# Four graph layers on one core: sums over features in quarters of the array, serial segment maxima, a softmax in two parts

## The chip, the core and the metric

The kernel runs on one core of a Trainium2 chip. The metric is the device time of one execution in microseconds (us); the number quoted is the median of three runs. TensorE appears as PE (matmuls) and PEld (weight loads), VectorE as DVE, ScalarE as ACT, GpSimd as POOL, SyncE as SP. Everything is float32 (f32), but for the operands of one matmul, which are float32r.

## The reference

The input `x` has 128 graphs of 64 nodes with 256 features each. Four layers follow one another, each as `x = layernorm(x + layer(x))`:

```python
# layer 0: dense attention over the 64 nodes of a graph
e = leaky(s1[:, :, None] + s2[:, None, :]); e = where(adj == 0, -inf, e)
h = softmax(e) @ Wh                       # Wh = x @ W, s1 = Wh @ a1, s2 = Wh @ a2
# layer 1: attention over 512 edges, 4 heads
e = einsum('behd,hd->beh', leaky(Xq[:, src] + Xq[:, dst]), a) + log(adj[src, dst] + eps)
m = segment_max(e, src); ex = exp(e - m[src])
attn = ex / segment_sum(ex, src)[src]
Y = segment_sum(attn * Xv[:, dst], src) @ W_out.T
# layer 2: graph convolution, then 256 -> 512 -> 256 with batch norm over all tokens
# layer 3: two graph convolutions, then LSTMs over windows of 1, 2, 3, 4 nodes
```

The change is in layers 0 and 1, and in the helper that normalises.

## The kernel before

The 128 graphs are cut in 16 blocks `q` of 8 graphs. A block is four tiles of 128 partitions, two graphs in each. A first long loop works through the blocks and does layers 0 and 1, and the first matmul of layer 2, in steps that are interleaved by hand: while block `q` passes through the edge attention (`l1_graph`, eight times, once per graph), block `q + 2` passes through layer 0 (`l0_a` to `l0_e`), block `q + 1` through its projections (`l1_t`, `l1_qv`), and block `q - 3` through the weighted sum and the output of layer 1 (`v_a`, `v_b`, `v_c`). The kernel is written against a layer that orders each engine's instructions itself and sets the semaphores; each engine then runs its own instructions strictly in that order.

For one graph `l1_graph` gathers the query sums of 512 edges by a matmul into `z` (L322; 128 features of a half on the partitions, 512 edges along the row), ACT applies a relu into `u` (L324), DVE joins the two halves with the signs of `a` (L325). `reduce_heads` (L312) then sums over the features, head by head: a matmul with a matrix `apad` that is zero but for four columns, so that the four head sums of this graph land on the right four of the 128 rows of one PSUM bank, `e`. The matmul is 128 columns wide although only four are not zero. Sixteen such matmuls, two blocks, fill the 16 x 4 = 64 used rows of `e`; the queue `pend` lets each run two graphs late (`DEEP = 2`).

Every two blocks (a softmax group `S`) `l1_softmax` adds the linear part of the scores (L335, a matmul with `spad`) and the edge bias, and finds the maximum over each segment of equal `src` along the row with two scans: one forward (`up`, L340), one backward (`dn`, L341), both over `e`, joined by a maximum (L342). After the exponential (L344) two more scans make the segment sums (L347, L348). PE transposes both results (L353), DVE divides (L357, L359), and four indirect DMAs (L363) from POOL's queue scatter the weights into a table in DRAM, from which the dense matrices `ld` are read back (L369). `v_a` rearranges them on POOL into `am` (L377) and multiplies them with the values in 64x64 corners of the array (L384).

In layer 0, `sb` (L227) is the column of scores `s2` broadcast along a row of 128, made on POOL; PE transposes it (L233), and DVE adds the other score and the mask into `lr` (L236) and takes the leaky relu into `e0` (L239).

`layernorm` takes statistics on DVE, computes the inverse root on POOL (L82), negates the mean into `ln_ng` on DVE (L94) and applies both in one instruction per row group on the given engine (L96). After the loop, the last three blocks' `v_a`, `v_b`, `v_c` are interleaved with layer 2's first matmuls (`up_block`, L684). The rest, layer 2's second half and layer 3 with its LSTMs, is some two thirds of the time and touched only through `layernorm`.

Of the kernel before, what the change touches and what calls it, by code (L numbers as in the profile page):

```python
# [8 lines left out]
F32 = mybir.dt.float32  # L9
F32R = mybir.dt.float32r  # L10
I32 = mybir.dt.int32
AF = mybir.ActivationFunctionType
# [5 lines left out]
P = 128  # L18
NB = 128
N = 64  # L20
# [9 lines left out]
GQ = 8  # L30
BPS = 2
SROWS = BPS * GQ * HEADS
PAIRS = N * N
SKIP = 4
NEG = -1.0e30
# [5 lines left out]
def kernel(ctx: ExitStack, tc: tile.TileContext, i, out):  # L41
# [42 lines left out]
    def layernorm(dst, src, n, engine):  # L84

        st = small.tile([P, n, 6], F32, name="ln_st", bufs=6)
        mv = small.tile([P, n, 2], F32, name="ln_mv", bufs=6)
        ng = small.tile([P, n], F32, name="ln_ng", bufs=6)
        rs = small.tile([P, n], F32, name="ln_rs", bufs=6)
        for r in range(n):  # L90
            nc.vector.bn_stats(st[:, r, :], src[:, r, :])
            nc.vector.bn_aggr(mv[:, r, :], st[:, r, :])
        rsqrt(rs, mv[:, :, 1], n)
        nc.vector.tensor_scalar_mul(ng, mv[:, :, 0], -1.0)  # L94
        for r in range(n):
            engine.tensor_scalar(dst[:, r, :], src[:, r, :], ng[:, r:r + 1], rs[:, r:r + 1],  # L96
                                 op0=OP.add, op1=OP.mult)


    bd = const.tile([P, P], F32, name="bd")  # L100
# [10 lines left out]
    with ExitStack() as two:  # L111
# [62 lines left out]

        mask = wa.tile([P, P], F32, name="mask")
        aht = wa.tile([P, P], F32, name="aht")
        apad = wa.tile([P, 2 * P - HEADS], F32, name="apad")
        same = wa.tile([P, 1], F32, name="same")
        gath = wa.tile([P, E], F32, name="gath")
        gath_r = wa.tile([P, E], F32R, name="gath_r")  # L180
# [35 lines left out]
        def l0_b(q):  # L216
            xT = L0[q]["xT"]
            wh = L0[q]["wh"] = own(q, [P, PQ, D + 2], "wh")
            for c in range(PQ):
                p_ = bank([D + 2])  # L220
                for k in range(KD):
                    nc.tensor.matmul(p_, xT[:, k, c * P:(c + 1) * P], w0[:, k, :],  # L222
                                     start=k == 0, stop=k == KD - 1)
                nc.scalar.activation(wh[:, c, :], p_, AF.Copy)

            sb = L0[q]["sb"] = own(q, [P, PQ, P], "sb")
            nc.gpsimd.tensor_copy(sb, wh[:, :, D + 1:].to_broadcast([P, PQ, P]))  # L227

        def l0_c(q):
            wh, sb = L0[q]["wh"], L0[q]["sb"]  # L230
            sc = bank([PQ, P])
            for c in range(PQ):
                nc.tensor.transpose(sc[:, c, :], sb[:, c, :], ident)  # L233
            t = own(q, [P, PQ, P], "lr")
            for c in range(PQ):
                nc.vector.scalar_tensor_tensor(t[:, c, :], sc[:, c, :], wh[:, c, D:D + 1], mask,  # L236
                                               op0=OP.add, op1=OP.add)
            e = L0[q]["e"] = work.tile([P, PQ, P], F32, name="e0")
            nc.vector.scalar_tensor_tensor(e, t, SLOPE, t, op0=OP.mult, op1=OP.max)  # L239
            mx = small.tile([P, PQ], F32, name="mx")  # L240
            nc.vector.tensor_reduce(mx, e, AX.X, OP.max, negate=True)
            sm = small.tile([P, PQ], F32, name="sm")
            for c in range(PQ):
                nc.scalar.activation(e[:, c, :], e[:, c, :], AF.Exp, bias=mx[:, c:c + 1],
                                     accum_out=sm[:, c:c + 1])
            ri = L0[q]["ri"] = small.tile([P, PQ], F32, name="ri")
            nc.vector.reciprocal(ri, sm)
# [31 lines left out]

        def l1_qv(q, c2):  # L280
            xT, v = L1[q]["xT"], L1[q]["v"]
            sp = spads[q // BPS % 2].rearrange("p (s b c h) -> p s b c h", s=4, b=BPS, c=PQ)
            pv = bank([2, D])
            for c in (2 * c2, 2 * c2 + 1):
                pq = bank([D + HEADS])
                for k in range(KD):
                    nc.tensor.matmul(pq, xT[:, k, c * P:(c + 1) * P], wq[:, k, :],  # L287
                                     start=k == 0, stop=k == KD - 1)
                for k in range(KD):
                    nc.tensor.matmul(pv[:, c % 2, :], xT[:, k, c * P:(c + 1) * P], wv[:, k, :],  # L290
                                     start=k == 0, stop=k == KD - 1)

                qs = work.tile([P, 2, D], F32R, name="qs", bufs=6)
                L1[q]["qs"].append(qs)
                for s in range(2):
                    r, ro = slice(s * N, (s + 1) * N), slice((1 - s) * N, (2 - s) * N)
                    nc.scalar.activation(qs[r, s, :], pq[r, :D], AF.Copy)  # L297
                    nc.vector.tensor_sub(qs[ro, s, :], pq[r, :D], qs[r, s, :].bitcast(F32))  # L298
                    nc.scalar.activation(sp[r, s, q % BPS, c, :], pq[r, D:], AF.Copy, scale=SLOPE)
            nc.scalar.activation(v[:, 2 * c2:2 * c2 + 2, :], pv, AF.Copy)  # L300

        pes, pend = {}, []
        DEEP = 2

        def reduce_heads(q, b, t):
            S = q // BPS
            c, s = divmod(b, 2)
            r0 = ((s * BPS + q % BPS) * PQ + c) * HEADS
            first = q % BPS == 0 and b == 0
            if first:  # L310
                pes[S] = bank([E], name="e", bufs=1)
            nc.tensor.matmul(pes[S], apad[:, P - HEADS - r0:2 * P - HEADS - r0], t, start=first, stop=False)  # L312

        def l1_graph(q, b):

# [4 lines left out]
            z = bank([KD, E], name="z", bufs=2)  # L320
            for k in range(KD):
                nc.tensor.matmul(z[:, k, :], L1[q]["qs"][c][:, s, k * P:(k + 1) * P], gath_r, start=True, stop=True)  # L322
            u = work.tile([P, KD, E], F32, name="u", bufs=4)
            nc.scalar.activation(u, z, AF.Relu)  # L324
            nc.vector.scalar_tensor_tensor(u[:, 0, :], u[:, 1, :], same, u[:, 0, :], op0=OP.mult, op1=OP.add)  # L325
            pend.append((q, b, u[:, 0, :]))
            if len(pend) > DEEP:
                reduce_heads(*pend.pop(0))

        ld = {}  # L330

        def l1_softmax(S):

# [3 lines left out]
            nc.vector.tensor_add(e, pe, lb)  # L337
            up = vp.tile([P, E], F32, name="up")
            dn = vp.tile([P, E], F32, name="dn")
            nc.vector.tensor_tensor_scan(up, seg[:, :E], e, NEG, OP.add, OP.max)  # L340
            nc.vector.tensor_tensor_scan(dn[:, ::-1], seg[:, 1:][:, ::-1], e[:, ::-1], NEG, OP.add, OP.max)  # L341
            nc.vector.tensor_max(up, up, dn)  # L342
            nc.vector.tensor_sub(e, e, up)
            nc.scalar.activation(e, e, AF.Exp)  # L344


            nc.vector.tensor_tensor_scan(up, keep, e, 0.0, OP.mult, OP.add)  # L347
            nc.vector.tensor_tensor_scan(dn[:, ::-1], seg[:, 1:][:, ::-1], up[:, ::-1], NEG, OP.add, OP.max)  # L348
            rows = []
# [4 lines left out]
                rows.append(p_)  # L354
            at = vp.tile([P, EC, SROWS], F32, name="at")
            rd = vp.tile([P, EC, SROWS], F32, name="rd")
            nc.vector.reciprocal(rd, rows[1][:, :, :SROWS])  # L357
            for c in range(EC):
                nc.vector.scalar_tensor_tensor(at[:, c, :], rows[0][:, c, :SROWS], count[:, c:c + 1], rd[:, c, :],  # L359
                                               op0=OP.mult, op1=OP.mult)  # L360

            for c in range(EC):
                nc.gpsimd.indirect_dma_start(  # L363
# [8 lines left out]
        def v_a(q):  # L372
            S, b = divmod(q, BPS)
            v = L1[q]["v"]
            am = vp.tile([P, PQ * HEADS, N], F32, name="am", bufs=2)
            w = PQ * HEADS
            nc.gpsimd.tensor_copy(am, ld[S][:, :, b * w:(b + 1) * w].rearrange("p n r -> p r n"))  # L377
            pY = [bank([KD, PQ, N]) for _ in range(2)]
            for c in range(PQ):
                for h in range(HEADS):  # L380
                    for s in range(2):
                        r = slice(s * N, (s + 1) * N)
                        r0 = (h % 2) * 64
                        nc.tensor.matmul(pY[s][r0:r0 + 64, h // 2, c, :], v[r, c, h * 64:(h + 1) * 64],  # L384
                                         am[r, c * HEADS + h, :], start=True, stop=True)
            yT = L1[q]["yT"] = vp.tile([P, KD, PQ, 2, N], F32, name="yT")
            for s in range(2):
                nc.scalar.activation(yT[:, :, :, s, :], pY[s], AF.Copy)
# [1 line left out]
        def v_b(q):  # L390
# [3 lines left out]
            for c2 in range(2):  # L394
# [3 lines left out]
                        nc.tensor.matmul(p_[:, c, :], yT[:, k, 2 * c2 + c].rearrange("p s n -> p (s n)"),  # L398
                                         wout[:, k, :], start=k == 0, stop=k == KD - 1)
                nc.vector.tensor_add(y[:, 2 * c2:2 * c2 + 2, :], p_, x1[:, 2 * c2:2 * c2 + 2, :])  # L400
            x2 = L1[q]["x2"] = vp.tile([P, PQ, D], F32, name="x2")
            layernorm(x2, y, PQ, nc.gpsimd)
            nc.sync.dma_start(x2_dram[q], x2.rearrange("p c d -> p (c d)"))

# [94 lines left out]
        def setup_signs():  # L499
# [1 line left out]
            nc.vector.tensor_scalar(acol, acol, 0.0, -2.0, op0=OP.is_lt, op1=OP.mult)  # L501
            nc.vector.tensor_scalar_add(acol, acol, 1.0)
            nc.vector.tensor_mul(same, acol[:, 0:1], acol[:, 1:2])
            nc.vector.tensor_scalar_mul(apad, iota_e[:, :2 * P - HEADS], 0.0)
            for h in range(HEADS):
                r, c0 = slice(h * 32, (h + 1) * 32), P - HEADS + h
                nc.vector.tensor_copy(apad[r, c0:c0 + 1], acol[r, 0:1])

        l0_a(0)
# [113 lines left out]
        for q in range(NQ):  # L623
# [10 lines left out]
            ]  # L634
            for b in range(GQ):
                some(l1_graph, q, b)
                if q and q % BPS == 0 and b == DEEP - 1:
                    l1_softmax(q // BPS - 1)
                for step, n, *more in between[b]:
                    some(step, n, *more)  # L640
                if setup:
                    setup.pop(0)()
        while pend:
            reduce_heads(*pend.pop(0))
        l1_softmax(NQ // BPS - 1)
        ph.close()


# [404 lines left out]
```

## Time and profile before

The median of three runs is 2236.68 us (2236.19 to 2237.63). The profiled execution spans 2237.3 us.

| what | value |
|---|---|
| PE busy | 2163.4 us (97%) |
| DVE busy | 926.0 us (41%) |
| ACT busy | 944.6 us (42%) |
| POOL busy | 435.0 us (19%) |
| chain that ended last: PE | 81% |
| chain that ended last: DVE, ACT | 9%, 5% |
| loop over blocks with all steps | about 60 to 595 us of the span |
| layer 2 and the LSTM part | from about 665 us on |

A group of instructions in the profile is given as line, engine, operation, output tile and input tiles, shapes and count; then busy time, mean duration in nanoseconds of one, and the idle time of the engine just before such instructions with what ended it. An f32 matmul appears as two instructions. Matmuls overlap their neighbours, so the durations of matmuls add up to more than the time they take; the distance from one start to the next is the honest price.

### The profile page before, as it was taken

What the parts mean: (1) busy time and instruction counts of PE and PEld (TensorE: products, weight loads), DVE (VectorE), ACT (ScalarE), POOL (GpSimd) and SP (SyncE); (2) the same over time, 40 slices, a digit from 0 to 9 for tenths busy, and PEclk for the clock granted to TensorE, in tenths of its full rate; (3) what the DMA queues carried; (4) which work ended last, traced back from release to release, by engine and by line L of the source; (5) the groups of instructions that cost most, each with busy time, mean ns of one, the idle gap of its engine ahead of it and who ended that gap; (6) DMA issues with size and microseconds to landing.
All of it is one profiled execution on the core that took longest, in us unless ns stands there. A gap on an engine that the chain in (4) does not pass through costs nothing.

```text
span 2237.3 us, 27559 instructions
## 1 busy us (share of the span) xinstructions
PE 2163.4 (97%) x10675; PEld 1411.7 (63%) x10675; DVE 926.0 (41%) x2136; ACT 944.6 (42%) x1821; POOL 435.0 (19%) x561
## 2 busy tenths in 40 slices
PE   5989999999899998999999999999999999999998
PEld 4667676666554444468468468468468468568467
DVE  7576756666544435232232323323323323323212
ACT  2655665656334802343343333333433433433333
POOL 1133334333320002011111111112112112112002
PEclk8999999999999998999999999999999999999999
DMA  4021233202223003000000000001001001000001
GB/s 121 19 40 29 50 50 51 50 32 39 41 41 111 19 0 104 0 20 29 29 20 29 29 19 29 29 20 29 29 19 29 28 20 29 19 10 29 10 0 29
DMA packets 129266, 74.46 MB, mean 33 GB/s; under 512 B 84976, under 2 KB 119920, under 8 KB 128880
## 3 DMA queue, kind: packets, MB, share of 16 engines
q1 hardware_dynamic: 124528, 70.74, 13.0%
q8 instruction: 84, 1.38, 0.3%
q10 hardware_dynamic: 3584, 0.92, 0.2%
q0 software_dynamic: 1024, 1.05, 0.2%
q14 instruction: 46, 0.38, 0.1%
HBM read 44.12 MB, written 28.57 MB: 32 GB/s over the span
## 4 chain that ended last, share of the span: by engine, by line
PE 81%; DVE 9%; ACT 5%; POOL 2%; DMA 1%; issue 1%; ACTq 0%; SPq 0%; POOLq 0%; DVEq 0%
PE l L927 34%; PE l L933 19%; PE pz L749 5%; PE pz L684 4%; DVE u L325 3%; PE g L867 2%; PE g L879 2%; PE e L312 2%; PE m L287 2%; PE m L222 2%; PE m L398 1%; PE g L829 1%; ACT u L324 1%; PE m L410 1%; PE m L290 1%
## 5 line engine op out<-in xcount | busy, mean ns | idle before, releaser
L927 PE MATMUL l<-H,wih 128*128 128x256 f32 (+2 forms) x2496 | 792.7, 470 | 0.8 <-ACT gate_g L947 0.5
L927 PEld LDWEIGHTS l<-H,wih 128*128 128x128 f32 x2496 | 467.7, 190 | 273.7 <-issue 179.4
L933 PE MATMUL l<-hid,whh 128*128 128x256 f32 (+2 forms) x1536 | 435.9, 437 | 0.0
L933 PEld LDWEIGHTS l<-hid,whh 128*128 128x128 f32 x1536 | 291.9, 190 | 128.4 <-issue 61.2
L939 ACT ACTIVATE gate_i<-l,bias 128x256 f32<-128x256 f32 (+2 forms) x176 | 100.0, 568 | 522.7 <-PE l L933 468.7
L942 DVE TENSOR_TENSOR gate_i<-gate_i,gate_g 128x256 f32<-128x256 f32 (+2 forms) x96 | 47.8, 498 | 580.8 <-ACT gate_g L939 580.8
L943 POOL TENSOR_TENSOR cell<-gate_f,cell 128x256 f32<-128x256 f32 (+2 forms) x96 | 83.6, 871 | 903.8 <-ACT gate_f L939 903.8
L82 POOL TENSOR_TENSOR ln_rs<-ln_rs,mhalf 128x2 f32<-128x2 f32 (+2 forms) x97 | 79.5, 819 | 498.7 <-DVE ln_ng L94 497.6
L324 ACT ACTIVATE u<-z 128x1024 f32<-128x1024 f32 x128 | 129.5, 1024 | 59.4 <-PE z L322 58.8
L312 PE MATMUL e<-u,apad 128*128 128x512 f32 x256 | 133.1, 606 | 11.3 <-DVE u L325 9.9
L939 ACT ACTIVATE gate_g<-l,bias 128x256 f32<-128x256 f32 (+2 forms) x176 | 100.1, 569 | 99.1 <-PE l L927 49.9
L325 DVE SCALAR_TENSOR_TENSOR u<-u,same 128x512 f32<-128x512 f32 x128 | 106.3, 841 | 57.8 <-ACT u L324 56.9
L939 ACT ACTIVATE gate_o<-l,bias 128x256 f32<-128x256 f32 (+2 forms) x176 | 99.2, 564 | 64.1 <-PE l L933 54.1
L946 DVE TENSOR_TENSOR cell<-gate_i,gate_g 128x512 f32<-128x512 f32 (+2 forms) x80 | 48.3, 603 | 156.1 <-ACT gate_g L939 155.6
L947 ACT ACTIVATE gate_g<-cell 128x256 f32<-128x256 f32 (+2 forms) x176 | 89.9, 511 | 52.9 <-DVE cell L946 38.4
L684 PE MATMUL pz<-A,w 128*128 128x512 f32 x256 | 112.1, 594 | 0.0
L322 PE MATMUL z<-gath_r,qs 128*128 128x512 f32 x256 | 106.9, 499 | 0.5 <-DVE qs L298 0.3
L684 PEld LDWEIGHTS pz<-A,w 128*128 128x128 f32 x256 | 48.1, 190 | 56.4 <-issue 54.3
L952 DVE TENSOR_TENSOR H<-gate_o,gate_g 128x512 f32<-128x512 f32 (+1 forms) x64 | 40.9, 639 | 89.0 <-PE l L927 71.4
L298 DVE TENSOR_TENSOR qs<-m,qs 64x256 fp32r<-64x256 f32 x128 | 54.1, 423 | 54.9 <-ACT qs L297 53.3
L939 ACT ACTIVATE gate_f<-l,bias 128x256 f32<-128x256 f32 (+2 forms) x96 | 51.0, 531 | 59.7 <-PE l L933 59.7
L287 PE MATMUL m<-wq,tT 128*128 128x260 f32 x256 | 71.2, 396 | 3.7 <-ACT tT L202 3.2
(240 smaller groups left out, 2674.8 us busy)
## 6 DMA issues: line engine op xcount, KB each, us to landing
xin<-in_x SPq DMA_DIRECT2D x16, 512.0 KB
ld<-table SPq DMA_DIRECT2D x16, 512.0 KB
x_dram<-x SPq DMA_DIRECT2D x16, 512.0 KB
x2r<-x_dram SPq DMA_DIRECT2D x32, 256.0 KB
x_dram<-A SPq DMA_DIRECT2D x64, 128.0 KB
x3r<-x_dram SPq DMA_DIRECT2D x64, 128.0 KB
out<-st SPq DMA_DIRECT2D x64, 128.0 KB
wih<-in_WihT SPq DMA_DIRECT2D x3, 1024.0 KB
```

The costliest lines, as they stand in the source:

```text
L287: nc.tensor.matmul(pq, xT[:, k, c * P:(c + 1) * P], wq[:, k, :], start=k == 0, stop=k == KD - 1)
L312: nc.tensor.matmul(pes[S], apad[:, P - HEADS - r0:2 * P - HEADS - r0], t, start=first, stop=False)
L322: nc.tensor.matmul(z[:, k, :], L1[q]["qs"][c][:, s, k * P:(k + 1) * P], gath_r, start=True, stop=True)
L324: nc.scalar.activation(u, z, AF.Relu)
L325: nc.vector.scalar_tensor_tensor(u[:, 0, :], u[:, 1, :], same, u[:, 0, :], op0=OP.mult, op1=OP.add)
L684: nc.tensor.matmul(p_, w1[:, k, m * P:(m + 1) * P], A[:, q, k * QT:(k + 1) * QT], start=k == 0, stop=k == KD - 1)
L749: nc.tensor.matmul(p_, w2[:, k, m * P:(m + 1) * P], hidden(q, k), start=k == 0, stop=k == M1 - 1)
L927: nc.tensor.matmul(gates[n], wih[p][:, k, mw * P:(mw + 1) * P], Hw[:, k, :, s, :], start=k == 0, stop=not s and k == KD - 1)
L933: nc.tensor.matmul(gates[n], whh[p][:, k, m * P:(m + 1) * P], hid[:, k], start=False, stop=k == KD - 1)
L939: nc.scalar.activation(act[n], gates[n], AF.Tanh if n == "g" else AF.Sigmoid, bias=bias[:, p - 1, m:m + 1])
L943: nc.gpsimd.tensor_tensor(cell[:, j], act["f"], cell[:, j], OP.mult)
L947: nc.scalar.activation(act["g"], cell[:, j], AF.Tanh)
```

## The change

Six edits are made together.

1. `reduce_heads` takes four graphs at once. Each of the four matmuls is 32 columns wide and writes its own 32 partitions of the bank `e`, so that the four use different quarters of the array's columns. `apad` shrinks, the rows of a group now lie in the first 16 partitions of each quarter, and what reads them (`spad`, `at`, `rd`, `am`, the indices in `v_a`) follows this order. The queue holds up to six graphs; `l1_graph` writes DVE's result to a tile `t` of its own with eight buffers, and `u` has three buffers in place of four.
2. `sb` is broadcast on ACT in place of POOL.
3. The segment maxima come from two scans in series: the backward scan runs over the result of the forward one, and the joining maximum goes.
4. `l1_softmax` ends after the exponential; the rest is `l1_weights`, called one graph later.
5. `layernorm` subtracts the mean itself, without `ln_ng`.
6. Tiles are saved: layer 0's `lr` and layer 1's `x2` are made in place, `am` has one buffer.

```diff
-            engine.tensor_scalar(dst[:, r, :], src[:, r, :], ng[:, r:r + 1], rs[:, r:r + 1],
-                                 op0=OP.add, op1=OP.mult)
+            engine.tensor_scalar(dst[:, r, :], src[:, r, :], mv[:, r, 0:1], rs[:, r:r + 1],
+                                 op0=OP.subtract, op1=OP.mult)
...
-            nc.gpsimd.tensor_copy(sb, wh[:, :, D + 1:].to_broadcast([P, PQ, P]))
+            nc.scalar.activation(sb, wh[:, :, D + 1:].to_broadcast([P, PQ, P]), AF.Copy)
...
-        def reduce_heads(q, b, t):
+        def reduce_heads(four):
+
+            q, b, t = four[0]
             S = q // BPS
-            c, s = divmod(b, 2)
-            r0 = ((s * BPS + q % BPS) * PQ + c) * HEADS
-            first = q % BPS == 0 and b == 0
-            if first:
+            if q % BPS == 0 and b == 0:
                 pes[S] = bank([E], name="e", bufs=1)
-            nc.tensor.matmul(pes[S], apad[:, P - HEADS - r0:2 * P - HEADS - r0], t, start=first, stop=False)
+
+            for q, b, t in reversed(four):
+                n, r0 = b % 2 * 2 + b // 2 % 2, (q % BPS * 2 + b // 4) * HEADS
+                nc.tensor.matmul(pes[S][n * CG:(n + 1) * CG, :], apad[:, CG - HEADS - r0:2 * CG - HEADS - r0], t,
+                                 start=r0 == 0, stop=False)
...
-            u = work.tile([P, KD, E], F32, name="u", bufs=4)
+            u = work.tile([P, KD, E], F32, name="u", bufs=3)
             nc.scalar.activation(u, z, AF.Relu)
-            nc.vector.scalar_tensor_tensor(u[:, 0, :], u[:, 1, :], same, u[:, 0, :], op0=OP.mult, op1=OP.add)
-            pend.append((q, b, u[:, 0, :]))
-            if len(pend) > DEEP:
-                reduce_heads(*pend.pop(0))
+            t = work.tile([P, E], F32, name="t", bufs=8)
+            nc.vector.scalar_tensor_tensor(t, u[:, 1, :], same, u[:, 0, :], op0=OP.mult, op1=OP.add)
+            pend.append((q, b, t))
+            if len(pend) == 4 + DEEP:
+                reduce_heads([pend.pop(0) for _ in range(4)])
...
             nc.vector.tensor_tensor_scan(up, seg[:, :E], e, NEG, OP.add, OP.max)
-            nc.vector.tensor_tensor_scan(dn[:, ::-1], seg[:, 1:][:, ::-1], e[:, ::-1], NEG, OP.add, OP.max)
-            nc.vector.tensor_max(up, up, dn)
-            nc.vector.tensor_sub(e, e, up)
+            nc.vector.tensor_tensor_scan(dn[:, ::-1], seg[:, 1:][:, ::-1], up[:, ::-1], NEG, OP.add, OP.max)
+            nc.vector.tensor_sub(e, e, dn)
             nc.scalar.activation(e, e, AF.Exp)
-
-
+            sm[S] = e, up, dn
+
+        def l1_weights(S):
+            e, up, dn = sm.pop(S)
             nc.vector.tensor_tensor_scan(up, keep, e, 0.0, OP.mult, OP.add)
...
-            am = vp.tile([P, PQ * HEADS, N], F32, name="am", bufs=2)
+            am = vp.tile([P, PQ * HEADS, N], F32, name="am")
...
-            x2 = L1[q]["x2"] = vp.tile([P, PQ, D], F32, name="x2")
+            x2 = L1[q]["x2"] = y
...
-                if q and q % BPS == 0 and b == DEEP - 1:
-                    l1_softmax(q // BPS - 1)
+                if q and q % BPS == 0 and b in (DEEP - 1, DEEP):
+                    (l1_softmax, l1_weights)[b - DEEP + 1](q // BPS - 1)
...
-        while pend:
-            reduce_heads(*pend.pop(0))
+        reduce_heads(pend)
         l1_softmax(NQ // BPS - 1)
+        l1_weights(NQ // BPS - 1)
```

More of the change, by code (lines that the diff above doesn't have):

```diff
@@ L32 @@
 SROWS = BPS * GQ * HEADS
+CG = P // PQ
 PAIRS = N * N
@@ L87, in layernorm @@
         mv = small.tile([P, n, 2], F32, name="ln_mv", bufs=6)
-        ng = small.tile([P, n], F32, name="ln_ng", bufs=6)
         rs = small.tile([P, n], F32, name="ln_rs", bufs=6)
@@ L93, in layernorm @@
         rsqrt(rs, mv[:, :, 1], n)
-        nc.vector.tensor_scalar_mul(ng, mv[:, :, 0], -1.0)
         for r in range(n):
-            engine.tensor_scalar(dst[:, r, :], src[:, r, :], ng[:, r:r + 1], rs[:, r:r + 1],
-                                 op0=OP.add, op1=OP.mult)
+            engine.tensor_scalar(dst[:, r, :], src[:, r, :], mv[:, r, 0:1], rs[:, r:r + 1],
+                                 op0=OP.subtract, op1=OP.mult)
     bd = const.tile([P, P], F32, name="bd")
@@ L176 @@
         aht = wa.tile([P, P], F32, name="aht")
-        apad = wa.tile([P, 2 * P - HEADS], F32, name="apad")
+        apad = wa.tile([P, 2 * CG - HEADS], F32, name="apad")
         same = wa.tile([P, 1], F32, name="same")
@@ L233, in l0_c @@
                 nc.tensor.transpose(sc[:, c, :], sb[:, c, :], ident)
-            t = own(q, [P, PQ, P], "lr")
+            e = L0[q]["e"] = work.tile([P, PQ, P], F32, name="e0")
             for c in range(PQ):
-                nc.vector.scalar_tensor_tensor(t[:, c, :], sc[:, c, :], wh[:, c, D:D + 1], mask,
+                nc.vector.scalar_tensor_tensor(e[:, c, :], sc[:, c, :], wh[:, c, D:D + 1], mask,
                                                op0=OP.add, op1=OP.add)
-            e = L0[q]["e"] = work.tile([P, PQ, P], F32, name="e0")
-            nc.vector.scalar_tensor_tensor(e, t, SLOPE, t, op0=OP.mult, op1=OP.max)
+            nc.vector.scalar_tensor_tensor(e, e, SLOPE, e, op0=OP.mult, op1=OP.max)
             mx = small.tile([P, PQ], F32, name="mx")
@@ L281, in l1_qv @@
             xT, v = L1[q]["xT"], L1[q]["v"]
-            sp = spads[q // BPS % 2].rearrange("p (s b c h) -> p s b c h", s=4, b=BPS, c=PQ)
+            sp = spads[q // BPS % 2].rearrange("p (s e x b d h) -> p s e x b d h", e=2, s=2, x=2, b=BPS, d=2)
             pv = bank([2, D])
@@ L298, in l1_qv @@
                     nc.vector.tensor_sub(qs[ro, s, :], pq[r, :D], qs[r, s, :].bitcast(F32))
-                    nc.scalar.activation(sp[r, s, q % BPS, c, :], pq[r, D:], AF.Copy, scale=SLOPE)
+                    nc.scalar.activation(sp[r, s, c % 2, 0, q % BPS, c // 2, :], pq[r, D:], AF.Copy, scale=SLOPE)
             nc.scalar.activation(v[:, 2 * c2:2 * c2 + 2, :], pv, AF.Copy)
@@ L322, in l1_graph @@
                 nc.tensor.matmul(z[:, k, :], L1[q]["qs"][c][:, s, k * P:(k + 1) * P], gath_r, start=True, stop=True)
-            u = work.tile([P, KD, E], F32, name="u", bufs=4)
+            u = work.tile([P, KD, E], F32, name="u", bufs=3)
             nc.scalar.activation(u, z, AF.Relu)
-            nc.vector.scalar_tensor_tensor(u[:, 0, :], u[:, 1, :], same, u[:, 0, :], op0=OP.mult, op1=OP.add)
-            pend.append((q, b, u[:, 0, :]))
-            if len(pend) > DEEP:
-                reduce_heads(*pend.pop(0))
-        ld = {}
+            t = work.tile([P, E], F32, name="t", bufs=8)
[3 more added lines that the diff above has]
+                reduce_heads([pend.pop(0) for _ in range(4)])
+        ld, sm = {}, {}
         def l1_softmax(S):
@@ L356, in l1_softmax @@
             rd = vp.tile([P, EC, SROWS], F32, name="rd")
-            nc.vector.reciprocal(rd, rows[1][:, :, :SROWS])
+            rd = rd.rearrange("p c (g r) -> p c g r", g=4)
+            used = [t.rearrange("p c (g x r) -> p c x g r", g=4, x=2)[:, :, 0] for t in rows]
+            nc.vector.reciprocal(rd, used[1])
             for c in range(EC):
-                nc.vector.scalar_tensor_tensor(at[:, c, :], rows[0][:, c, :SROWS], count[:, c:c + 1], rd[:, c, :],
-                                               op0=OP.mult, op1=OP.mult)
+                nc.vector.scalar_tensor_tensor(at[:, c, :].rearrange("p (g r) -> p g r", g=4), used[0][:, c],
+                                               count[:, c:c + 1], rd[:, c], op0=OP.mult, op1=OP.mult)
             for c in range(EC):
@@ L374, in v_a @@
             v = L1[q]["v"]
-            am = vp.tile([P, PQ * HEADS, N], F32, name="am", bufs=2)
-            w = PQ * HEADS
-            nc.gpsimd.tensor_copy(am, ld[S][:, :, b * w:(b + 1) * w].rearrange("p n r -> p r n"))
+            am = vp.tile([P, PQ * HEADS, N], F32, name="am")
+            nc.gpsimd.tensor_copy(am.rearrange("p (e r) n -> p e r n", e=2),
+                                  ld[S].rearrange("p n (e b r) -> p b e r n", e=2, b=BPS)[:, b])
             pY = [bank([KD, PQ, N]) for _ in range(2)]
@@ L384, in v_a @@
                         nc.tensor.matmul(pY[s][r0:r0 + 64, h // 2, c, :], v[r, c, h * 64:(h + 1) * 64],
-                                         am[r, c * HEADS + h, :], start=True, stop=True)
+                                         am[r, (c % 2) * 2 * HEADS + c // 2 * HEADS + h, :], start=True, stop=True)
             yT = L1[q]["yT"] = vp.tile([P, KD, PQ, 2, N], F32, name="yT")
@@ L503, in setup_signs @@
             nc.vector.tensor_mul(same, acol[:, 0:1], acol[:, 1:2])
-            nc.vector.tensor_scalar_mul(apad, iota_e[:, :2 * P - HEADS], 0.0)
+            nc.vector.tensor_scalar_mul(apad, iota_e[:, :2 * CG - HEADS], 0.0)
             for h in range(HEADS):
-                r, c0 = slice(h * 32, (h + 1) * 32), P - HEADS + h
+                r, c0 = slice(h * 32, (h + 1) * 32), CG - HEADS + h
                 nc.vector.tensor_copy(apad[r, c0:c0 + 1], acol[r, 0:1])
```

## The prediction

> **What bounds the kernel now.** I read the page first, then the stretches of the layer 0/1 loop, then what TensorE waited for there, then its instructions in order of time. The page says that TensorE is nearly always occupied.
>
> ```profile
> PE 2163.4 (97%) x10675; PEld 1411.7 (63%) x10675; DVE 926.0 (41%) x2136; ACT 944.6 (42%) x1821; POOL 435.0 (19%) x561
> ...
> L312 PE MATMUL e<-u,apad 128*128 128x512 f32 x256 | 133.1, 606 | 11.3 <-DVE u L325 9.9
> ```
>
> L312, the sum over features (`reduce_heads`), is 256 instructions: 128 calls, each split in two. The change rebuilds just this. It lies in the loop over blocks, which the stretches show (columns: busy PE, PEld, DVE, ACT, POOL, clock, DMA share, GB/s):
>
> ```profile
> 199.00:265.00 66.00, 62.80 (x412) 47.24 (x411) 42.23 (x102) 39.38 (x92) 22.07 (x25) 1.00 0.29 51
> 331.00:397.00 66.00, 63.51 (x400) 45.96 (x399) 45.67 (x107) 38.72 (x85) 26.01 (x28) 1.00 0.28 51
> 463.00:530.00 67.00, 64.56 (x410) 46.92 (x411) 44.69 (x105) 40.28 (x89) 22.64 (x24) 1.00 0.25 42
> ```
>
> PE is about 96% busy, DVE 64 to 69%, ACT about 60%. So what leaves PE here leaves the time, until another engine or a latency takes over. The waits of PE between 265 and 530 us are small:
>
> ```profile
> PE e L312 <- DVE u L325: 2.7, 4, 0.7
> PE m L233 <- POOL sb L227: 2.3, 4, 0.7
> PE m L410 <- issue: 2.1, 4, 0.5
> PE m L287 <- ACT tT L202: 1.0, 4, 0.2
> PE m L353 <- DVE dn L348: 0.7, 4, 0.2
> ```
>
> In order of time one reads the period and the true prices, start to start (a modelled 592 ns duration overlaps its successor):
>
> ```profile
> 265.13 1.02 PE L335 MATMUL e<-gath,spad 128*128 128x512 f32 x2
> ...
> 335.93 1.02 PE L335 MATMUL e<-gath,spad 128*128 128x512 f32 x2
> ...
> 406.86 1.02 PE L335 MATMUL e<-gath,spad 128*128 128x512 f32 x2
> ```
>
> One softmax group (two blocks) takes 71 us. And:
>
> ```profile
> 640.95 1.16 PE L384 MATMUL m<-am,v 64*64 64x64 f32 x64 [0.54 <-POOL am L377]
> 642.04 2.84 PE L684 MATMUL pz<-A,w 128*128 128x512 f32 x6
> 644.72 3.62 PE L398 MATMUL m<-wout,yT 128*128 128x256 f32 x16
> 648.17 7.03 PE L684 MATMUL pz<-A,w 128*128 128x512 f32 x16
> 655.04 1.95 PE L410 MATMUL m<-aht,x 128*128 128x128 f32 x16
> ```
>
> A 512-column f32 instruction costs 6.87/16 = 0.429 us (648.17 to 655.04), a 256-column one 3.45/16 = 0.216. L384 uses quarters of the array (64x64): at 0.216/4 = 0.054 each, its 64 would take 3.45 us one by one, yet the next line starts after 1.09. So matmuls in different corners of the array do overlap here, 3.2-fold, switching of the array's shape included.
>
> **What the Trainium skill says.** "TensorE: Matmul & The Clock Gate", Part 3 (Packing small matmuls), states that outputs in different 32-partition strips let matmuls run side by side, three column tiles of 512 columns measured 2.38 times faster. No 128x32 matmul is in this trace; L384 agrees in kind. "TensorEngine Tiling (Array Packing)", Tiling Modes, says that a change of tiling mode drains TensorE; the 1.09 us of L384 holds both its drains. "PSUM — Partial Sum Buffer", in its passages on bank collisions, says that column tiles may write disjoint partitions of one bank at the same time, which the new `e` bank needs; no trace of before shows it.
>
> **The change part by part.**
>
> *Sums in quarters.* Before: 128 calls x 2 x 0.429 = 110 us of PE. After: 32 groups of four 32-column calls. If four overlap as L384 does, a group costs 8 x 0.429 / 3.2 = 1.07 us against 3.43, saving 2.36, 75 us in all. Per softmax group (four of them) that is 9.4 us of 71. Lower bound of the saving: the two instructions of a call sit on the same quarter; if the second must end before the next call can pass it, a group takes 5 x 0.429 + about 0.24 for the shape changes = 2.38 and saves 1.05, 34 us in all. (The 0.24: 1.09 less 64 x 0.054 / 4 = 0.86.) I take the first, because L384 is also made of calls split in two and overlaps fully.
>
> *Queue of six instead of three, eight buffers for `t`.* A sum now comes four to six blocks after its `t`. PE's wait of 2.7 us per 265 on L325, 0.7 per softmax group, mostly goes.
>
> *Broadcast of `sb` on ACT.* The POOL copy (0.606 us each) becomes an ACT copy of 512 elements, 0.60 us by the row of L411 (597 ns). ACT grows by 1.2 us per 71, beside PE work. In return `sb` no longer queues on POOL behind the indirect DMA starts; the 2.3 us on L233 (0.6 per softmax group) go.
>
> *Scans in series, softmax in two parts.* `tensor_max` (0.68 us on DVE) goes: the backward scan runs over the forward one. In the new instruction order DVE runs the chain without the `t` operations between: 0.68 + 1.22 + 1.22 + 0.68, exponential with its handovers about 1.1, 1.21 + 1.23: about 7.3 us from the end of the sum's last matmul to `dn`. PE has until its transposes of `dn` only its L222 group (3.46), the 64 small matmuls (1.09), one z pair (0.46) and the transposes of `e` (0.44), some 5.4. So it waits about 2 us per softmax group. Behind these transposes stand the next z matmuls, hence ACT's relu and DVE's `t`. This is the new wait.
>
> *Smaller edits.* Without `ln_ng` a normalisation drops 0.16 us of DVE; PE bounds the LSTM part, so nothing there. One `am` buffer: the second copy waits for the first's matmuls and what follows it on POOL is the normalisation that follows those matmuls anyway. Norm in place (`x2` is `y`): the next `y` comes a block later, the DMA out has that long. `e0` in place, `apad` shorter: no time. I cost all these at zero.
>
> *Sum.* PE leaves 9.4 per softmax group, old waits 0.7 + 0.6 go, the new one costs 2.0, and I take off 0.7 since ACT and DVE would then be at some 70 and 75% in strict order: 71 falls by 8.0. Six full groups (121.8 to 548, between the L335 starts): 48. The first group (to 121.8) still carries the setup on DVE: half, 4.5. The last (548 to 594) has eight of its sixteen sums in a run where ACT's relu, 1.02 us a step, becomes the limit instead of 1.32 us a step: 8 x 0.3 = 2.4, plus four to five for the others less their share of waits, in all 6. After 594 the pace is set by the last softmax, its table and the L684 work laid beside it, which no edit shortens by more than the 0.7 of `tensor_max`. Total 58.5: 2236.7 - 58.5 = 2178.
>
> **The rivals.**
>
> *The relief lands in full.* The new DVE chain's wait is hidden, and the 5.6 us per softmax group that PE loses now shrink too: 75 + about 10 = 85 us, 2152. For it: DVE is not full. Against: the strict order of the chain above.
>
> *A latency takes over or the overlap is partial.* By POOL's and PE's order of time, 37.8 us pass from L335 at 265.13 to the end of the first `am` copy at 302.9 (softmax, four indirect DMAs, table load, copy), and PE comes to use it at 306.56. With two groups of sums fewer before it (4.7 us) PE comes after 36.7, the chain, without the five `t` between its scans, lasts about 35.5. This margin of about 1 us may be overrun; or the quarter pairs overlap by halves (34 us of saving). Either gives 25 to 35 us in all: 2202 to 2212.
>
> *No overlap: not faster.* Then 32 shape changes are added to 110 us unchanged: 32 x 0.24 = 8 us, 16 us of new waits on `dn`, less about 10 of waits gone: 2250. Against: L384.
>
> **How the numbers follow.** Forecast 0.62, full relief 0.15, latency or partial overlap 0.16, no overlap 0.07. The range goes from 2152 (full relief) to 2210, within the partial case; under and over it about 2 in 10 remain. Faster 0.93, same 0.02, slower 0.05, since even the last case can come out below 2232.
>
> **What would show it.** The new 32-column matmuls: 8 starts per group in about 1.07 us, four starting almost together; 2.4 would be the partial case, 3.4 none. The period between the spad matmuls near 63 us. PE's largest wait in the loop on DVE `dn`. The part from the LSTM on unchanged within a few microseconds. I am wrong if `am`'s DMA chain or ACT's queue becomes PE's main releaser, or if the period stays at 68 or more.

## The result

The changed kernel takes 2272.26 us (2271.18 to 2273.73, four runs) against 2236.76 us before: a ratio of 1.0159, 95% interval 1.0141 to 1.0176. It is slower by 35 us where 58 us of gain were forecast. The profiled execution spans 2270.7 us. From its page, the busy times and the instruction that applies the normalisation (L96 before, L95 now):

```profile
PE 2132.6 (94%) x10675; PEld 1389.7 (61%) x10675; DVE 907.7 (40%) x2031; ACT 950.5 (42%) x1837; POOL 577.9 (25%) x545
...
L95 POOL TENSOR_SCALAR A<-xin,ln_mv,ln_rs 128x256 f32<-128x256 f32 x64 | 88.8, 1398 | 1.7
...
L95 POOL TENSOR_SCALAR y<-y,ln_mv,ln_rs 128x256 f32<-128x256 f32 x64 | 81.3, 1279 | 1.8
L95 POOL TENSOR_SCALAR st<-x3r,ln_mv,ln_rs 128x256 f32<-128x256 f32 x64 | 77.9, 1226 | 3.4
L95 POOL TENSOR_SCALAR A<-x2r,ln_mv,ln_rs 128x256 f32<-128x256 f32 x64 | 77.8, 1225 | 3.3
```

POOL grew from 435.0 to 577.9 us, although the copy of `sb` left it. The four groups above add up to 325.8 us; the groups of the POOL engine before show what they were:

```profile
L96 POOL TENSOR_SCALAR A<-xin,ln_ng,ln_rs 128x256 f32<-128x256 f32 x64 | 64.2, 1016 | 1.7
L96 POOL TENSOR_SCALAR A<-x2r,ln_ng,ln_rs 128x256 f32<-128x256 f32 x64 | 38.1, 605 | 3.3
L96 POOL TENSOR_SCALAR x<-y,ln_ng,ln_rs 128x256 f32<-128x256 f32 x64 | 37.0, 588 | 1.8
L96 POOL TENSOR_SCALAR st<-x3r,ln_ng,ln_rs 128x256 f32<-128x256 f32 x64 | 36.2, 574 | 3.4
```

175.5 us for the same 256 instructions. The median of one is 0.55 us with an addition and 1.23 us with a subtraction. In the loop this is what PE waits for. The waits of PE from 265 to 540 us after the change (total, times, longest):

```profile
PE m L392 <- POOL am L384: 24.3, 4, 6.1
PE m L359 <- ACT u L326: 7.4, 4, 1.9
PE m L418 <- issue: 2.2, 5, 0.5
PE m L359 <- ACT wh L223: 1.7, 4, 0.4
PE m L418 <- POOL y L95: 1.6, 3, 0.5
```

Why `am` is late is seen in order of time, first on POOL, then on PE:

```profile
281.85 5.62 POOL L95 TENSOR_SCALAR y<-y,ln_mv,ln_rs 128x256 f32<-128x256 f32 x4
295.88 1.03 POOL L83 TENSOR_TENSOR ln_rs<-ln_rs,mhalf 128x4 f32<-128x4 f32 x1 [8.41 <-DVE ln_rs L82]
297.02 5.18 POOL L95 TENSOR_SCALAR A<-xin,ln_mv,ln_rs 128x256 f32<-128x256 f32 x4
302.16 1.90 POOL L384 COPY am<-ld 128x1024 f32<-128x1024 f32 x1
```

```profile
296.77 1.28 PE L324 MATMUL z<-gath_r,qs 128*128 128x512 f32 x4
304.11 1.99 PE L392 MATMUL m<-am,v 64*64 64x64 f32 x64 [6.06 <-POOL am L384]
```

The copy of `am` stands behind layer 0's four normalisation instructions in POOL's queue, and these now last 5.2 us. The same place in e1 (below: all edits but this one):

```profile
286.30 2.16 POOL L97 TENSOR_SCALAR A<-xin,ln_ng,ln_rs 128x256 f32<-128x256 f32 x4
288.41 1.96 POOL L386 COPY am<-ld 128x1024 f32<-128x1024 f32 x1
```

The norm delays `am` a second time, through the load that `am` copies from. In SP's queue the load of `ld` stands behind the DMA that writes layer 1's `y` out, and this one waits for the norm of `y` (the 5.62 us above; 2.68 us in e1). SP after the change, then in e1:

```profile
287.50 0.34 SPq L411 DMA_DIRECT2D x_dram<-y  x1
287.95 4.01 SPq L377 DMA_DIRECT2D ld<-table  x2
```

```profile
276.36 0.34 SPq L413 DMA_DIRECT2D x_dram<-y  x1
276.80 4.00 SPq L379 DMA_DIRECT2D ld<-table  x2
```

Counted from the spad matmuls of the same softmax group (258.01 and 249.06 us), the load is issued after 29.9 us in place of 27.7, and the copy of `am` ends after 46.1 us in place of 41.3.

PE is idle for 6.06 us; in e1 it waits 0.6 us here. Then 64 matmuls take 1.92 us to the next start where 1.09 was usual: the granted clock has fallen. The stretches of the loop say how often (columns: busy PE, PEld, DVE, ACT, POOL, clock, DMA share, GB/s):

```profile
331.00:397.00 66.00, 56.45 (x392) 43.23 (x391) 41.55 (x92) 39.31 (x91) 33.31 (x26) 0.92 0.29 51
463.00:530.00 67.00, 57.63 (x406) 43.90 (x406) 43.60 (x100) 41.06 (x90) 29.80 (x23) 0.92 0.24 42
```

The clock was 1.00 here before. From 265 to 540 us the trace's clock records show two stretches of half clock in each softmax group: one of 6.8 us, which begins in the last 3 us of the wait on `am`, and one of 3.4 us, which begins within 0.6 us of the end of a wait of 1.85 us before the transposes of `dn` (L359; the profile puts this wait down to ACT's `u`, which in the first of them ends 0.14 us behind the scan of `dn`). All stretches that begin between 60 and 690 us, called the loop's half clock below, add up to 81.9 us, against 6.8 before. The Trainium skill, "TensorE: Matmul & The Clock Gate", Part 1, says that the clock is halved after an idle window of about 3.4 us; the steps of 3.4 and 6.8 us agree with that length.

The length of a wait alone doesn't decide it, though. In e1 PE waits for `dn` four times between 250 and 460 us, 1.79 to 2.07 us each; half clock begins at the waits that end at 258.36 and 388.06 us, and not at those that end at 323.50 and 453.20. The stretches of e1 around the second and the third (same columns) show it:

```profile
265.00:331.00 66.00, 61.01 (x440) 45.22 (x439) 47.37 (x112) 43.92 (x99) 24.34 (x27) 1.00 0.28 51
331.00:397.00 66.00, 61.50 (x437) 46.13 (x430) 47.28 (x113) 43.98 (x100) 23.25 (x26) 0.97 0.27 52
```

In every trace the half-clock stretches begin whole multiples of 3.413 us apart, and last 1 to 7 such steps (but for the last one, which the program's end cuts). Where a wait falls on this grid may decide; no run tests it.

### The profile page after: what moved, and what is told of

Its sections match the earlier page's. It is cut to its first block, busy times and chain, and to the rows that moved or that the text cites. A ratio compares the mean times of both kernels' runs of the same rounds, so it can differ in the third digit from the quotient of the medians.

```text
span 2270.7 us, 27396 instructions
## 1 busy us (share of the span) xinstructions
PE 2132.6 (94%) x10675; PEld 1389.7 (61%) x10675; DVE 907.7 (40%) x2031; ACT 950.5 (42%) x1837; POOL 577.9 (25%) x545
## 4 chain that ended last, share of the span: by engine, by line
PE 73%; issue 9%; POOL 8%; DVE 5%; ACT 4%; DMA 1%; POOLq 0%; ACTq 0%; DVEq 0%
PE l L935 30%; PE l L941 18%; PE pz L757 5%; POOL A L95 3%; PE pz L692 3%; PE g L875 2%; PE g L887 2%; POOL y L95 2%; PE m L406 2%; POOL ln_rs L83 2%; PE g L837 1%; ACT u L326 1%; PE m L286 1%; PE z L324 1%; PE e L313 1%
## 5 line engine op out<-in xcount | busy, mean ns | idle before, releaser
L328 DVE SCALAR_TENSOR_TENSOR t<-u,same 128x512 f32<-128x512 f32 x128 | 98.9, 776 | 58.1 <-ACT u L326 56.1
L324 PE MATMUL z<-gath_r,qs 128*128 128x512 f32 x256 | 99.6, 484 | 5.1 <-ACT u L326 4.6
L95 POOL TENSOR_SCALAR A<-xin,ln_mv,ln_rs 128x256 f32<-128x256 f32 x64 | 88.8, 1398 | 1.7
L95 POOL TENSOR_SCALAR y<-y,ln_mv,ln_rs 128x256 f32<-128x256 f32 x64 | 81.3, 1279 | 1.8
L95 POOL TENSOR_SCALAR st<-x3r,ln_mv,ln_rs 128x256 f32<-128x256 f32 x64 | 77.9, 1226 | 3.4
L95 POOL TENSOR_SCALAR A<-x2r,ln_mv,ln_rs 128x256 f32<-128x256 f32 x64 | 77.8, 1225 | 3.3
```

The costliest lines, as they stand in the source:

```text
L95: engine.tensor_scalar(dst[:, r, :], src[:, r, :], mv[:, r, 0:1], rs[:, r:r + 1], op0=OP.subtract, op1=OP.mult)
L328: nc.vector.scalar_tensor_tensor(t, u[:, 1, :], same, u[:, 0, :], op0=OP.mult, op1=OP.add)
```

## The experiments

Every run is compared with the kernel before on the same chip, whose median there was 2238.5 to 2240.0 us. An edit also changes the order in which the instructions are laid out, so differences of some microseconds between versions aren't a pure price of the edited line.

**Is it the norm?** Two runs turn the normalisation alone, in both directions.

```diff
 # e1: changed kernel, norm of before
-                                 op0=OP.subtract, op1=OP.mult)      # scalar mv[:, r, 0:1]
+        nc.vector.tensor_scalar_mul(ng, mv[:, :, 0], -1.0)
+                                 op0=OP.add, op1=OP.mult)           # scalar ng = -mean
 # e2: kernel before, norm of the change: the same lines the other way
```

> The changed kernel with the normalisation of before (negated mean, add). Theory N (the norm that subtracts is slow on POOL, and its chain holds PE up): POOL norms fall from 1226 to about 550 ns, PE's wait on am and on the norms in the LSTM part goes, clock back near 0.99; 2165 to 2195 us. Rival L (the new softmax order, the single am buffer and the relu queue hold PE up whatever the norm costs): the layer 0/1 loop still ends near 584 us, only the LSTM part comes back by about 23 us; 2240 to 2255 us.

> The kernel before with only the normalisation changed (subtract, no negated mean). Theory N: POOL norms at about 1226 ns, the LSTM part longer by about 23 us, the loop longer too as norms stand before the am copy on POOL; 2265 to 2320 us. Rival L: only the LSTM part suffers, and the loop is unchanged; 2255 to 2262 us. If the norm is slow only together with the in-place tile: 2237 us.

e1: 2196.19 us, ratio 0.9806 (0.979 to 0.9823). e2: 2302.31 us, ratio 1.0281 (1.0263 to 1.0298). So the norm costs the changed kernel 76 us, and the kernel before 63 us. Rival L falls in e1, in which the loop comes back too: its last spad matmul is at 546.8 us in place of 583.6. In e2 the loop suffers as well, as theory N has it: its last spad matmul is at 619 us in place of 594, and PE waits 17.8 us for `sb` in place of 4.3, which in that kernel is queued on POOL as well.

**The operation, or where its scalar lies?**

```diff
 # e3: changed kernel; the mean is first copied to ng
+        nc.vector.tensor_scalar_mul(ng, mv[:, :, 0], 1.0)
+            engine.tensor_scalar(dst[:, r, :], src[:, r, :], ng[:, r:r + 1], rs[:, r:r + 1], op0=OP.subtract, op1=OP.mult)
 # e4: changed kernel; the mean is negated in place
+        nc.vector.tensor_scalar_mul(mv[:, :, 0], mv[:, :, 0], -1.0)
+            engine.tensor_scalar(dst[:, r, :], src[:, r, :], mv[:, r, 0:1], rs[:, r:r + 1], op0=OP.add, op1=OP.mult)
 # e15: x * rs - mean * rs
+        nc.vector.tensor_mul(ng, mv[:, :, 0], rs)
+            engine.tensor_scalar(dst[:, r, :], src[:, r, :], rs[:, r:r + 1], ng[:, r:r + 1], op0=OP.mult, op1=OP.subtract)
```

> The changed kernel with the mean copied to a tile of its own and then subtracted. If the subtraction as operation is what is slow: norms at about 1226 ns, 2265 to 2280 us. If it is the scalar read from every second word of the statistics: norms at about 550 ns, 2165 to 2195 us.

> The changed kernel with the mean negated in place in the statistics tile and then added from there. The reverse of the run before: about 550 ns and 2165 to 2195 us if the operation is the cause, about 1226 ns and 2265 to 2280 us if it is where the scalar is read from.

> The changed kernel with the norm as x * rs - mean * rs on POOL: a subtraction again, but as second operation. If any subtraction makes POOL's two-step operation slow: norms at about 1226 ns, 2260 us or more. If only a subtraction in first place does: about 550 ns, 2195 to 2215 us, as the DVE product now waits for POOL's root.

e3: 2270.71 us, ratio 1.0137 (1.0117 to 1.0158); e4: 2195.16 us, 0.98 (0.978 to 0.982); e15: 2306.96 us, 1.0305 (1.0284 to 1.0326). One line of each, from the view of the norm's source line (count, then minimum, median and maximum in ns), in the order e3, e4, e15:

```profile
L97 POOL TENSOR_SCALAR A<-x2r,ln_ng,ln_rs x64: 1222/1226/1229, 860.7 to 2035.2; 128x256 f32<-128x256 f32 x64
```

```profile
L96 POOL TENSOR_SCALAR y<-y,ln_mv,ln_rs x64: 545/556/1448, 171.7 to 637.9; 128x256 f32<-128x256 f32 x64
```

```profile
L97 POOL TENSOR_SCALAR A<-x2r,ln_rs,ln_ng x64: 1212/1222/1530, 886.5 to 2070.8; 128x256 f32<-128x256 f32 x64
```

With the subtraction in first place the instruction is slow wherever the scalar lies (e3 and the changed kernel), and with the addition there it is fast wherever the scalar lies (e1, e4). e15 is slow with the subtraction in second place, but it has the multiplication in first; no run has a multiplication first and an addition second, so that e15 alone doesn't say which of the two slows it. Its time doesn't compare with e3's either: the added product on DVE stands between POOL's root and the norm.

**Which of the other edits gain?** All with the old norm.

```diff
 # e7: changed kernel; broadcast on POOL as before
-            nc.scalar.activation(sb, wh[:, :, D + 1:].to_broadcast([P, PQ, P]), AF.Copy)
+            nc.gpsimd.tensor_copy(sb, wh[:, :, D + 1:].to_broadcast([P, PQ, P]))
 # e10: changed kernel; both maximum scans over e, as before
-            nc.vector.tensor_tensor_scan(dn[:, ::-1], seg[:, 1:][:, ::-1], up[:, ::-1], NEG, OP.add, OP.max)
-            nc.vector.tensor_sub(e, e, dn)
+            nc.vector.tensor_tensor_scan(dn[:, ::-1], seg[:, 1:][:, ::-1], e[:, ::-1], NEG, OP.add, OP.max)
+            nc.vector.tensor_max(up, up, dn)
+            nc.vector.tensor_sub(e, e, up)
 # e8: changed kernel; softmax in one part
-                if q and q % BPS == 0 and b in (DEEP - 1, DEEP):
-                    (l1_softmax, l1_weights)[b - DEEP + 1](q // BPS - 1)
+                if q and q % BPS == 0 and b == DEEP - 1:
+                    l1_softmax(q // BPS - 1)
+                    l1_weights(q // BPS - 1)
 # e13: changed kernel; the second part one graph later still
+                if q and q % BPS == 0 and b in (DEEP - 1, DEEP + 1):
+                    (l1_softmax, l1_weights)[b - DEEP + 1 >> 1](q // BPS - 1)
```

e5 is the changed kernel with the edits of e7, e10 and e8 together: of the change only `reduce_heads` in quarters, its queue and the tiles in place are left. e6 is the kernel before with those three parts of the change, and with `e`, `x2` and `am` in place or in one buffer, but without the quarters and their queue.

> Only the sums in quarters, with the queue and the tiles saved to make room; norm, POOL broadcast, parallel scans with their maximum and the softmax in one part as before. Theory Q (the gain of 43 us of the changed kernel with the old norm is the quarters' relief, and the other edits are worth little): 2190 to 2205 us. Rival S (softmax and broadcast edits are needed to let the relief through): 2210 to 2235 us.

> The kernel before with the ACT broadcast, the serial scans, the softmax in two parts and the tiles in place, but with sums of full width and the old norm. Theory Q: 2232 to 2242 us, no measurable change. Rival S: 2220 us or less, as these edits carry part of the gain.

> The changed kernel with the old norm and the softmax left in one part. If the wait on dn, 2 us per softmax group, is bound to the chain of scans itself: 2194 to 2200 us, as with two parts (2196). If the later call of the second part is what delays the table and PE's use of it: 2185 us or less.

> The changed kernel with the old norm and the broadcast of sb back on POOL. If POOL's queue (indirect DMA starts) is what held sb back and PE's wait on it: 5 to 15 us more than 2196, so 2201 to 2211. If ACT is the tighter engine after the change: 2185 to 2196 us.

> The changed kernel with the old norm and both maximum scans over e again, joined by tensor_max. The chain to dn is 0.68 us longer, so PE waits 0.68 us more per softmax group: 2199 to 2204 us with the clock's share. If the scans are hidden: 2196 us.

> The changed kernel with the old norm and the softmax's second part called one graph later still, so that a z pair and the transposes of sb stand before the transposes of e and dn on PE. If the wait on dn and the clock after it are what keeps the gain at 43 us instead of 58: 2180 to 2192 us. If the table's chain to am then comes too late: PE's wait on am grows, 2196 to 2210 us.

| run | us | ratio (95%) | against e1 |
|---|---|---|---|
| e1, all edits, old norm | 2196.19 | 0.9806 (0.979 to 0.9823) | |
| e5, quarters only | 2233.43 | 0.9977 (0.9968 to 0.9987) | +37.2 |
| e6, all but quarters | 2224.75 | 0.994 (0.9923 to 0.9956) | +28.6 |
| e8, softmax in one part | 2220.21 | 0.9911 (0.9894 to 0.9927) | +24.0 |
| e7, broadcast on POOL | 2207.35 | 0.9854 (0.9838 to 0.9871) | +11.2 |
| e10, parallel scans | 2209.58 | 0.9861 (0.9844 to 0.9877) | +13.4 |
| e13, second part later | 2207.3 | 0.9854 (0.9837 to 0.987) | +11.1 |

Theory Q falls: PE is relieved in e5 as in e1, but only 6 us of it reach the end. The edits depend on one another. Alone the quarters bring 6 us, on top of the others 28.6. No run takes the saved tiles and buffers (edit 6, `u` with three) back by themselves. The waits of e5 from 200 to 560 us show where the relief went:

```profile
PE z L326 <- ACT u L328: 11.2, 20, 1.4
PE m L362 <- DVE dn L357: 9.1, 4, 2.9
PE m L234 <- POOL sb L228: 8.1, 7, 2.9
```

In a strict order PE has less of its own work to cover a relu, a chain of scans or a broadcast; each becomes a wait. In addition the clock falls: 58.0 us of half clock in the loop of e5, 54.6 in e8 and in e10, against 37.5 in e1.

Some of these runs came out otherwise than expected. e8 and e10 are slower than either of their branches allows, and e6 falls between its two. e13 lies in the range of its second branch, but not by its reason: PE's wait on `am` isn't there from 200 to 550 us, and PE waits 9.5 us for DVE's `t` instead. In e7 the time is as expected, but PE waits on `am` (7.7 us in that window, 3.6 in e1) and not on `sb`. So the table says what an edit is worth beside the others; by which wait is not shown.

**Does the half clock cost time of its own?** Matmuls without use were put into the waits, into banks that are overwritten afterwards.

```diff
 # e11: changed kernel as it is (slow norm), in v_a; e12 and e14: e1, in l1_weights before the transposes of dn
+            for _ in range(6 if b == 0 and S < NQ // BPS - 1 else 0):
+                nc.tensor.matmul(pY[0].rearrange("p k c n -> p (k c n)"), ident, gath, start=True, stop=True)
...
+                for _ in range(2 if row is dn else 0):      # e14: 1
+                    nc.tensor.matmul(p_.rearrange("p c t -> p (c t)"), ident, gath, start=True, stop=True)
```

> The changed kernel as it is, with the slow norm, and six matmuls more without use before the weighted sum of each even block but the last group's, in a bank that is overwritten afterwards: 7 x 12 instructions of 0.429 us, 36 us of PE work put where PE waits about 6 us for am. If the low granted clock after this wait (0.92 in the loop) costs time of its own: the clock in the loop rises and the time falls, to 2245 to 2268 us. If the clock's falls cost nothing, as PE waits anyway: 2272 us or up to 15 us more.

> The changed kernel with the old norm, and two matmuls without use (four instructions of 0.429 us) between the transposes of e and of dn, where PE waits about 2 us per softmax group. If half-clock stretches after this wait cost time of their own (37.5 us of half clock in the loop, 18.8 us of full clock lost): clock in the loop up, 2180 to 2192 us. If only the waits count: 2196 us or up to 3 more.

> As the run with two matmuls without use before the transposes of dn, but with one (two instructions, 0.86 us), so that it ends before dn is ready and does not push the table's chain back. If the half clock after the wait on dn costs time of its own: 2183 to 2193 us, with less half clock in the loop than 37.5 us. If the half clock costs nothing, or one matmul is too little to keep the clock up: 2194 to 2200 us.

e11: 2261.57 us, 1.0103 (1.0086 to 1.0119): with some 36 us more work on PE (84 instructions of 0.429 us) it is 10.7 us faster than the changed kernel. Half clock in the loop falls from 81.9 to 23.9 us. This speaks for a cost of the low clock beside the waits, but it is no pure price: PE's order changed too (the sums in quarters no longer stand between the 64 small matmuls and layer 1's output matmuls). e12: 2208.08 us (0.9859, 0.9843 to 0.9875), e14: 2203.4 us (0.9841, 0.9825 to 0.9857): half clock falls from 37.5 to 23.9 and 13.7 us, and yet both are slower than e1, and than either branch had it. In e12 PE's order of time shows that the filler itself waits for its bank and ends behind the time at which `dn` is there:

```profile
258.62 0.66 PE L363 MATMUL m<-ident,e 128*128 128x128 f32 x4 [0.51 <-ACT wh L225]
259.77 1.98 PE L361 MATMUL m<-gath,ident 128*128 128x512 f32 x4 [0.49 <-ACT yT L400]
261.59 0.60 PE L363 MATMUL m<-ident,dn 128*128 128x128 f32 x4
```

The transposes of `dn` start 9.5 to 9.8 us behind the spad matmuls in place of e1's 9.3, and what follows from them, the table and `am`, is pushed back. In e14 they start after 9.2 us, so there the filler doesn't push the chain back; yet PE waits longer for the relu (10.7 us from 200 to 550 us, 7.4 in e1) and for `am` (5.7, against 3.6). Why isn't shown. So in these two less half clock brought no time, and what the low clock costs by itself stays open.

## Why the prediction was wrong

**The step that failed** is "Smaller edits", the sentence on `ln_ng`, costed at zero. It looked at the DVE instruction that went, and at PE as the bound of the LSTM part, and took the POOL instruction that stayed for unchanged. It was another operation. From 0.55 to 1.23 us each, 256 of them: POOL does 150 us more, of which e1 shows 76 us on the path. In its place the changed kernel shows PE waiting 6.06 us on `am` in each of four softmax groups, where e1 has 0.6. Compared with e1, the span of the changed kernel (77.2 us longer in the two profiles) divides so, by PE's first and last starts: loop to the last spad matmul 36.8 us, from there to layer 2's second matmuls 11.2, to the first LSTM matmul 5.8, the rest 23.4. In the rest PE was said to be the bound, and so nothing could be lost there; the waits after 870 us say otherwise:

```profile
PE g L837 <- POOL A L95: 14.1, 14, 2.7
PE l L837 <- POOL A L95: 1.0, 2, 0.5
```

Twice in each of seven groups the graph convolution's matmuls stand in PE's queue before the LSTM's, and wait for the norm. Twelve of these waits, 10.9 us, lie behind the first LSTM matmul, where e1 has none. Half clock there grows from 7.3 to 23.0 us, by estimate 7.8 us more at half speed. Together this is 18.7 of the 23.4 us; the rest is open.

Two of the forecast's own signs of being wrong came true: `am` is PE's main releaser in the loop, and the period stays at 70.3 us (six groups from 122.6 to 544.6 us).

The other steps can be judged by e1, which has all edits but this one:

- *Quarters overlap as the 64x64 corners do*: right. Forecast 1.07 us a group of four; from the changed kernel's order of time:

```profile
329.20 1.07 PE L313 MATMUL e<-t,apad 128*32 128x512 f32 x8
330.19 1.12 PE L338 MATMUL e<-gath,spad 128*128 128x512 f32 x2
```

  0.99 us from start to start; the first four of the eight start within 0.02 us, the other four 0.45 us behind them.
- *The old waits on L325 and on `sb` mostly go*: right. From 200 to 550 us e1 has one wait of 2.4 us for `t`, and none for `sb`.
- *A new wait on `dn` of 2 us*: right. In e1, again in order of time, with the next spad matmuls for the period:

```profile
249.06 1.12 PE L340 MATMUL e<-gath,spad 128*128 128x512 f32 x2
...
314.15 1.12 PE L340 MATMUL e<-gath,spad 128*128 128x512 f32 x2
...
323.50 0.63 PE L361 MATMUL m<-ident,dn 128*128 128x128 f32 x4 [2.06 <-DVE dn L356]
...
378.73 1.13 PE L340 MATMUL e<-gath,spad 128*128 128x512 f32 x2
```

- *A softmax group at 63.0 us*: mis-sized. e1 has 64.7 on average (119.1 to 507.4 us, six groups), so the six bring 38 us, not 48. For ACT and DVE in strict order the sum took off 0.7 us a group, and for `am` nothing. The waits of e1 from 200 to 550 us:

```profile
PE z L326 <- ACT u L328: 7.4, 10, 1.1
PE m L394 <- POOL am L386: 3.6, 5, 1.2
PE m L408 <- DVE rd L367: 1.0, 2, 0.5
```

  Together they are about 2 us a group. That these make up the difference is an account of the waits, not shown by a run. The half clock of 37.5 us in e1's loop overlaps with it, and e12 and e14 don't separate the two: this stays open.
- *The first group and the last*: e1 has 2.7 us for the forecast 4.5, and 6.9 for 6.
- *The tail after the last softmax group unchanged*: 4.0 us longer in e1 (148.5 us in place of 144.5 to layer 2's second matmuls).
- *The rival of a late `am`* named the right wait, with a margin of about 1 us. It was put down to the softmax chain. In e1 this margin is overrun by 0.6 us; the other 5.5 us of the changed kernel come with the norm, ahead of `am` in POOL's queue and, by way of `y`, ahead of its load in SP's. The forecast asked what stands behind `am` on POOL, and not what stands before it.
- *The rival of full relief* rests on 5.6 us that PE loses in each softmax group. The stretches shown there, 95 to 96% busy, leave about 3 of 71 us, and no line shows the rest.

The faster version is among the runs: e1 and e4, 2196 and 2195 us, beat both kernels.

## What to carry to other kernels

An edit that saves an instruction by changing the operation of another is a change of that other's price. Where the profile has no line for the new operation on that engine, put a lowest and a highest price on it, however small the edit. An engine at a fifth of its time can still set the end where its queue stands between a transfer and its first use; price what is ahead in that queue, and what is ahead of the transfer in its own. And relief for the bound engine reaches the end only as far as the waits around it have cover; here four edits had to come together.

## What the runs showed of the hardware

POOL's two-step operation with two scalars per partition, 128x256 f32, has a median of 0.55 us with add and multiply (e1, e4), of 1.23 us with subtract and multiply (e3, the changed kernel) and of 1.22 us with multiply and subtract (e15), wherever the scalar lies in the first two. Four 128x32 f32 matmuls of 512 columns, eight instructions, run in 0.99 us; four of full width take 3.43 by estimate (8 x 0.429). PE's half clock comes on a grid of 3.413 us: stretches begin and last whole multiples of it in every trace. In the changed kernel it came at waits of 1.85 and of 6.06 us, in e1 at two of four waits of about 2 us. Useless matmuls in the waits of 6 us went with 10.7 us less time, those in the waits of 2 us with 7 and 12 us more.
